# Making the four result fetches of a row wait for each other's landing, in a four-layer kernel's first attention

## The chip, the cores and the metric

The kernel runs on one core of a Trainium2 chip. The metric is the device time of one execution in microseconds (us); the time given for a kernel is the median of its runs.

## The reference, cut to what matters

The input `x` has 16 rows of 256 channels by 512 positions, and `cond` is a 16 x 512 array of zeros and ones. Four layers are added to `x` in turn: an attention with 8 heads (`L0`), a causal convolution along the channel axis with `cond` as its taps, a recurrent layer (a gated cell, 256 steps), and an attention with 16 heads. The first attention is the one of this document:

```python
x = x + _L0_cond_ref(x, cond_2048, L0_cond_Wq, L0_cond_Wo)      # this one
x = x + _L1_cond_ref(x, cond_2048[:, None, :])
x = x + _L2_cond_ref(cond_2048, x, L2_cond_W_ih, L2_cond_W_hh, L2_cond_b_ih, L2_cond_b_hh)
x = x + _L3_cond_ref(x, cond_2048, L3_cond_Wq, L3_cond_Wk, L3_cond_Wv, L3_cond_b)

# inside L0, with cmask/rmask from the mask's columns and rows
logits = (scores * cmask + (1.0 - cmask) * NEG) * rmask
ctx = softmax(logits) @ qh          # keys and values are the queries: one projection
out = ctx @ Wo.T
```

A position whose mask is 0 is never attended to, and as a query it takes the plain mean over all positions. So each row needs its attention only over its positions with mask 1 (under 288 of the 512 here), and one more result, the mean's, for all the others.

## The kernel before

The first attention (`attend0_together`) works on one row (one `b` of 16) after another, packed: it gathers the positions with mask 1 to the front, attends among them, and gives every position its result back. The order of instructions on every engine comes from a planner: each step is added to a plan with an engine, an estimated duration and a place, and the plan puts out a fixed order per engine. Each engine then runs its list in that order, and waits on semaphores where the data asks for it. Rows overlap: while the last steps of row `b` run, the first steps of a later row run between them.

The steps of a row, with their lines:

- `gather`. SyncE loads the row (`xA`, L842). TensorE turns it (L853), ScalarE copies it into `xT` (L857), and POOL sends its positions in four indirect DMAs of 128 positions each to their packed places in a table in HBM (`table<-xT,togo`, L310, function `send`). SyncE fetches the packed table back (`xsA`, L320 and L322). TensorE turns that (L880), projects it (L827, a helper that several products share) and makes values (L914). POOL also makes a mask of places, `uA` (L923).
- `group`, twice, for four heads each. Scores for the row maxima (L938), maxima on VectorE (L945, L950), maxima brought into place by four small DMAs (`whh<-whh`, L957), scores again (L981), exponentials on ScalarE (L990, L993), the weighing (L1011 and L827). The sums of weights go to HBM (L1037).
- `divide`. The sums are loaded (L1041), inverted, stored (L1044), and spread over partitions by eight DMAs (`pbA`, L1051). POOL multiplies the two halves of the context `cxA` by them (L1054).
- `finish`. TensorE multiplies by the output weights (L827 with `woT`), ScalarE copies (L1086), SyncE writes the row's packed results to HBM in two parts (`result<-ocA`, L1091). When both are there, POOL fetches for every position the result that belongs to it, in four indirect DMAs of 128 positions and 128 KB each (`backA<-result,goto`, L1098). VectorE adds all four to `xT` (L1101). Then the first part of the convolution is made from the row's new values: POOL copies them (`early`, L567), VectorE multiplies and sums (L573 to L575).

The plan's order on POOL around the fetches of a row is: four fetches, first scaling of the next row's `cxA`, two sends of a later row, second scaling, third send, `uA`, `early`, fourth send, and then the next row's fetches. From row 10 on there are no sends left. On the SyncE queue, L320 of a later row comes ahead of the two L1091 of the current row.

```python
for f in range(NT):
    outs.append(plan.add("POOL", 1.3, put + (outs[-1:] or [rs_.take(r)]), lambda f=f: nc.gpsimd.indirect_dma_start(
        R4[r.i][:, f], None, results[b], bass.IndirectOffsetOnAxis(goto[:, f, b : b + 1], 0))))
landed = plan.add("LAG", 2.5, outs, lambda: None)
```

In the plan each fetch follows the one before, but only in order: on the chip POOL issues the next as soon as it has issued this one. `R4` (`backA`) has two buffers.

Of the kernel before, what the change touches and what calls it, by code (L numbers as in the profile page):

```python
# [18 lines left out]
B, D, T = 16, 256, 512  # L19
# [245 lines left out]
def tile_kernel(ctx: ExitStack, tc: tile.TileContext, x, cond, Wq0, Wo0, W_ih, W_hh, b_ih, b_hh,  # L265
                Wq3, Wk3, Wv3, b3, consts, out, cols):
    nc = tc.nc
# [296 lines left out]
    def early(b, w, xs, products):  # L564

        if w == 0:
            yield "POOL", 0.7, lambda: nc.gpsimd.tensor_copy(xs[:, :, TAPS - 1 :], xT[:, :, b, 0 : EARLY * PART])  # L567
        a = xs[:, :, w * PART : w * PART + TAPS].unsqueeze(2).broadcast_to([P, NT, PART, TAPS])
        steps = [list(d) for d in a.ap]
        steps[2][0] = 1  # L570
        every = bass.AP(tensor=a.tensor, offset=a.offset, ap=steps)
        y = yw[w // 2][:, :, b, w % 2 * PART : (w % 2 + 1) * PART]
        yield "DVE", 1.3, lambda: nc.vector.tensor_tensor(products, every, condT.unsqueeze(2).broadcast_to([P, NT, PART, TAPS]), ALU.mult)  # L573
        yield "DVE", 1.3, lambda: nc.vector.tensor_reduce(y, products, AX.X, ALU.add)
        yield "DVE", 0.2, lambda: nc.vector.tensor_tensor(y, y, xs[:, :, TAPS - 1 + w * PART : TAPS - 1 + (w + 1) * PART], ALU.add)  # L575
# [155 lines left out]
    def attend0_together():  # L731
# [8 lines left out]
        with ExitStack() as es:  # L740
            work = es.enter_context(tc.tile_pool(name="workA", bufs=1))
            pp = es.enter_context(tc.tile_pool(name="psumA", bufs=1, space=PSUM))
            plan = Plan()
# [28 lines left out]
            def tiles(name, n, shape, space=work):  # L772
                return plan.slots(n), [space.tile(shape, F32, tag=f"{name}{i}", name=f"{name}A{i}") for i in range(n)]
# [20 lines left out]
            rs_, R4 = tiles("back", 2, [P, NT, D])  # L794
            results = [nc.dram_tensor(f"result{b}", (ROOM + 1, D), F32, kind="Internal").ap() for b in range(B)]
            goto = work.tile([P, NT, B], U32, tag="goto", name="goto")
# [26 lines left out]
            def wide(to, left, right, start, stop):  # L823

                n = left.shape[1]
                for r in range(0, n, R):
                    nc.tensor.matmul(to[r : min(n, r + R)], lhsT=left[:, r : min(n, r + R)], rhs=right, start=start, stop=stop, skip_group_check=True)  # L827
# [244 lines left out]
            def finish(b, g0, cx, done):  # L1072

                plan.lay(PLACES["finish"], g0)
                oc, made, put, products = ocs.new(), [], [], []
                for part in range(2):
                    sm = banks.new()

                    def product(part=part, sm=sm):
                        for c in range(2) if part == 0 else [2]:  # L1080
                            r = P if c < 2 else TAILK + 1
                            for g in range(GQ):
                                wide(SM[0:r, sm.i][:, (c % 2) * D : (c % 2 + 1) * D], CX[cx.i][:, g, c * P : c * P + r], woT[:, g, :], g == 0, g == GQ - 1)
                    m = plan.add("PE", 1.71 if part == 0 else 0.86, done + [banks.take(sm)] + ([] if part else [ocs.take(oc)]) + made, product, mode="c32")
                    products.append(m)
                    c = plan.add("ACT", 0.6 if part == 0 else 0.38, [m], lambda part=part, sm=sm: nc.scalar.copy(  # L1086
                        OC[oc.i][:, 0:2].rearrange("p c d -> p (c d)") if part == 0 else OC[oc.i][0 : TAILK + 1, 2],
                        SM[0 : P if part == 0 else TAILK + 1, sm.i][:, 0 : (2 - part) * D]))
                    banks.free(sm, c)
                    made.append(c)  # L1090
                    put.append(plan.add("SP", 3.0, [c], lambda part=part: nc.sync.dma_start(  # L1091
                        out=results[b][0 : 2 * P].rearrange("(c p) d -> p c d", p=P) if part == 0 else results[b][2 * P :],
                        in_=OC[oc.i][:, 0:2] if part == 0 else OC[oc.i][0 : TAILK + 1, 2])))
                cs.free(cx, *products)
                ocs.free(oc, *put)
                r, outs = rs_.new(), []
                for f in range(NT):
                    outs.append(plan.add("POOL", 1.3, put + (outs[-1:] or [rs_.take(r)]), lambda f=f: nc.gpsimd.indirect_dma_start(  # L1098
                        R4[r.i][:, f], None, results[b], bass.IndirectOffsetOnAxis(goto[:, f, b : b + 1], 0))))
                landed = plan.add("LAG", 2.5, outs, lambda: None)  # L1100
                outs = [plan.add("DVE", 1.22, [landed], lambda: nc.vector.tensor_tensor(  # L1101
                    xT[:, :, b], xT[:, :, b], R4[r.i], ALU.add))]
                rs_.free(r, *outs)
                ea, n = ears.new(), None
                for w in range(EARLY if b < B - 1 else 1):
                    for engine, dur, f in early(b, w, *ear):
                        n = plan.add(engine, dur, [n] if n else outs + [ears.take(ea)], f)
                ears.free(ea, n)
                return put
# [9 lines left out]
            for b in range(B):  # L1119
                g0 = GQ * b  # L1120
                v, heads, v_done, turned, u = gather(b, g0)
                cx, done, totals, weighed = cs.new(), [], [], []
                opened = cs.take(cx)
                for g in range(GQ):
                    c, opened, last, tot, summed = group(g, b, g0 + g, heads[g], v, v_done, turned, cx, opened, u)
                    done.append(c)
                    totals.append((tot, summed))
                    weighed.append(last)
                vs.free(v, *weighed)
                us.free(u, *weighed)  # L1130
                put = finish(b, g0, cx, (divide if b < B - 1 else closing)(b, g0, cx, done, totals))
# [643 lines left out]
```

## Time and profile before

| what | value |
|---|---|
| timed runs, us | 2384.07, 2382.76, 2374.28; median 2382.76 |
| the profiled execution's own time | 2376.67 us |
| its span, first to last instruction | 2374.9 us |
| mean granted TensorE clock | 0.971 |
| first attention, fetches of rows 0 to 12 | from 109.34 to 418.40 us |
| fetches of the last three rows | from 440.74 to 467.10 us |
| recurrent layer | until about 1560 us |

How to read it: the profile is one execution. An engine's busy time is the sum of its instructions; semaphores, branches and the issuing of DMAs by SyncE are not in it. For POOL's indirect DMAs the busy time is that of writing the descriptors, about 1 us each, and the data moves after it. The view of waits says for how long an engine stood idle just before an instruction, and which instruction or DMA ended that. The view of the chain goes back from the last instruction, each time to what released it.

### The profile page before, as it was taken

What the parts mean: (1) busy time and instruction counts of PE and PEld (TensorE: products, weight loads), DVE (VectorE), ACT (ScalarE), POOL (GpSimd) and SP (SyncE); (2) the same over time, 40 slices, a digit from 0 to 9 for tenths busy, and PEclk for the clock granted to TensorE, in tenths of its full rate; (3) what the DMA queues carried; (4) which work ended last, traced back from release to release, by engine and by line L of the source; (5) the groups of instructions that cost most, each with busy time, mean ns of one, the idle gap of its engine ahead of it and who ended that gap; (6) DMA issues with size and microseconds to landing.
All of it is one profiled execution on the core that took longest, in us unless ns stands there. A gap on an engine that the chain in (4) does not pass through costs nothing.

```text
span 2374.9 us, 105954 instructions
## 1 busy us (share of the span) xinstructions
PE 2207.9 (93%) x47074; PEld 1460.0 (61%) x47074; DVE 1688.3 (71%) x4639; ACT 995.9 (42%) x2648; POOL 414.0 (17%) x402
## 2 busy tenths in 40 slices
PE   5999999569999999999999999959999999999994
PEld 4555555358989988988898988833333333333331
DVE  2377778768888888888888855666666666666651
ACT  3545544223333333333333333215555555555542
POOL 3244443300000000000000000030332242232113
PEclk8999999789999999999999999989999999999997
DMA  6223322500000000000000000010111111111001
GB/s 202 73 80 89 101 62 63 167 3 4 9 4 5 5 5 5 5 5 4 5 5 5 5 4 4 4 38 15 45 44 32 41 41 40 32 46 36 22 22 40
DMA packets 70166, 83.91 MB, mean 35 GB/s; under 512 B 28808, under 2 KB 48842, under 8 KB 69700
## 3 DMA queue, kind: packets, MB, share of 16 engines
q1 hardware_dynamic: 60484, 60.09, 8.4%
q0 software_dynamic: 9216, 16.96, 2.4%
q8 instruction: 371, 6.08, 1.0%
q14 instruction: 95, 0.78, 0.1%
HBM read 48.58 MB, written 35.98 MB: 36 GB/s over the span
## 4 chain that ended last, share of the span: by engine, by line
PE 88%; DVE 3%; DMA 2%; issue 2%; ACT 2%; POOL 1%; SPq 1%; another core or an unknown queue 0%; POOLq 0%; DVEq 0%; ACTq 0%
PE pr L1211 11%; PE smC L1472 10%; PE pn L1211 9%; PE pz L1211 9%; PE smC L1606 7%; PE smA L827 6%; PE smC L1638 6%; PE smC L1663 5%; PE pt L1202 5%; PE pr L1190 4%; PE pz L1190 4%; PE smA L981 3%; PE smA L1011 3%; PE smA L938 2%; PE smA L853 1%
## 5 line engine op out<-in xcount | busy, mean ns | idle before, releaser
L1613 DVE TENSOR_REDUCE nmC<-smC 128x2 f32<-128x576 f32 x512 | 362.5, 750 | 178.7 <-PE smC L1606 162.2
L310 POOL DMA_INDIRECT table<-xT,togo x128 | 128.1, 1001 | 1239.8 <-DVE whh L1482 1077.3
L1211 PE MATMUL pr<-whh,hist 128*32 128x128 f32 x8192 | 282.8, 275 | 41.7 <-DVE hist L1274 28.9
L1649 ACT ACTIVATE wih<-smC 128x1024 f32<-128x1024 f32 x256 | 251.8, 1023 | 150.4 <-PE smC L1638 149.8
L1211 PEld LDWEIGHTS pr<-whh,hist 128*32 128x32 f32 x8192 | 220.2, 110 | 125.7 <-issue 40.0
L1211 PE MATMUL pz<-whh,hist 128*32 128x128 f32 x8192 | 280.9, 273 | 0.8 <-issue 0.8
L1211 PE MATMUL pn<-whh,hist 128*32 128x128 f32 x8192 | 280.1, 273 | 0.0
L555 DVE SCALAR_TENSOR_TENSOR yw<-xT,condT,yw 128x512 f32<-128x512 f32 x360 | 269.2, 748 | 5.5
L1211 PEld LDWEIGHTS pz<-whh,hist 128*32 128x32 f32 x8192 | 238.6, 110 | 1.6 <-issue 1.2
L1211 PEld LDWEIGHTS pn<-whh,hist 128*32 128x32 f32 x8192 | 238.3, 110 | 0.1
L1190 PE MATMUL pr<-wih,xw 128*32 128x128 f32 x4096 | 225.4, 273 | 3.1 <-issue 3.0
L1190 PE MATMUL pz<-wih,xw 128*32 128x128 f32 x4096 | 226.4, 273 | 1.6 <-issue 1.1
L1245 ACT ACTIVATE nn<-pre 128x64 f32<-128x64 f32 x256 | 65.7, 257 | 385.5 <-DVE pre L1242 385.5
L1606 PE MATMUL smC<-kC,qC 32*128 32x288 f32 x2048 | 200.5, 453 | 7.8 <-ACT wih L1649 2.6
L1606 PEld LDWEIGHTS smC<-kC,qC 32*128 32x128 f32 x2048 | 83.6, 183 | 197.0 <-DVE nmC L1613 82.4
L1236 ACT ACTIVATE r<-pr 128x128 f32<-128x128 f32 x256 | 70.9, 277 | 282.5 <-PE pr L1211 274.7
L1638 PE MATMUL smC<-qC,kC 32*128 32x512 f32 x1024 | 168.2, 638 | 0.2
L1202 PE MATMUL pt<-xw,wih 128*32 128x256 f32 x2048 | 167.7, 379 | 0.1
L1703 POOL TENSOR_TENSOR aC<-aC,pbC 128x512 f32<-128x512 f32 x64 | 81.4, 1279 | 491.3 <-DMA pbC<-sums 420.3
L1190 PEld LDWEIGHTS pz<-wih,xw 128*32 128x32 f32 x4096 | 143.9, 110 | 6.5 <-issue 6.3
L1190 PEld LDWEIGHTS pr<-wih,xw 128*32 128x32 f32 x4096 | 142.9, 110 | 6.2 <-issue 5.6
L1237 DVE STREAM_TRANSPOSE rT<-r 128x128 f32<-128x128 f32 x256 | 78.6, 307 | 76.2 <-ACT r L1236 74.2
(184 smaller groups left out, 3420.8 us busy)
## 6 DMA issues: line engine op xcount, KB each, us to landing
xA<-in_x_dram SPq DMA_DIRECT2D x16, 512.0 KB
pbC<-sums SPq DMA_DIRECT2D x256, 32.0 KB
out_dram<-oC SPq DMA_DIRECT2D x32, 256.0 KB
table<-zeros SPq DMA_DIRECT2D x16, 288.0 KB
pbA<-totals SPq DMA_DIRECT2D x120, 36.0 KB
xsA<-table SPq DMA_DIRECT2D x16, 256.0 KB
result<-ocA SPq DMA_DIRECT2D x16, 256.0 KB
xsC<-table SPq DMA_DIRECT2D x16, 256.0 KB
```

The lines of the kernel that those rows point to most:

```text
L310: one = nc.gpsimd.indirect_dma_start(tables[b], bass.IndirectOffsetOnAxis(togo[:, f, b : b + 1], 0), xT[:, f, b], None, bounds_check=ROOM ...
L555: nc.vector.scalar_tensor_tensor(acc, xT[:, f, :, lo : lo + WIN], condT[:, f, k : k + 1], xT[:, f, :, t0 : t0 + WIN] if k == 0 else acc, A ...
L827: nc.tensor.matmul(to[r : min(n, r + R)], lhsT=left[:, r : min(n, r + R)], rhs=right, start=start, stop=stop, skip_group_check=True)
L1190: nc.tensor.matmul(sets[k % 2][0 if g == GATE_R else 2][32 * j : 32 * j + 32].rearrange("p (f i) -> p f i", i=32), lhsT=x2, rhs=gates(wih, ...
L1202: nc.tensor.matmul(ps[32 * j : 32 * j + 32], lhsT=wih[:, kc, 2 * T + fo * P + 32 * j : 2 * T + fo * P + 32 * j + 32], rhs=parts[p][:, kc]. ...
L1211: nc.tensor.matmul(ps[32 * j : 32 * j + 32].rearrange("p (f i) -> p f i", i=32), lhsT=slot[:, f], rhs=gates(whh, f, j)[:, g], start=False, ...
L1472: nc.tensor.matmul(to[R3 * j : R3 * j + R3], lhsT=left[:, R3 * j : R3 * j + R3], rhs=right, start=start, stop=stop)
L1606: nc.tensor.matmul(SM[:, st[j].i, 0:ROOM], lhsT=Q[qt.i][R * j : R * j + R, qc * P : (qc + 1) * P], rhs=K[kt.i][R * j : R * j + R, 0:ROOM], ...
L1613: nc.vector.tensor_reduce(NM[nm.i][:, qc, lo : lo + len(some)], SM[:, some[0] : some[-1] + 1, 0:ROOM], AX.X, ALU.max, negate=True)
L1638: nc.tensor.matmul(SM[:, st[j].i], lhsT=K[kt.i][r, kc * P : kc * P + P], rhs=Q[qt.i][r, :], start=True, stop=True)
L1649: nc.scalar.activation(E[e.i][:, lo : lo + len(some)], SM[:, some[0] : some[-1] + 1], AF.Exp)
L1663: nc.tensor.matmul(SM[R * j : R * j + R, acc.i], lhsT=V[v.i][:, c, 8 * (g // 2) + 2 * j + q], rhs=E[held[c].i][:, j], start=(c == 0), stop ...
```

## The change

The four fetches of a row get a wait. Each but the first is made to depend on the landing of the one asked for before it, in rows 0 to 12; in rows 13, 14 and 15 nothing changes. The plan's steps, durations and places are the same, and so is the order of all instructions on every engine; what differs in the built program are the semaphores that these POOL instructions wait for.

```diff
                 r, outs = rs_.new(), []
+                fetched = []
+
+                def bring(f):
+                    one = nc.gpsimd.indirect_dma_start(R4[r.i][:, f], None, results[b], bass.IndirectOffsetOnAxis(goto[:, f, b : b + 1], 0))
+                    if fetched and b < B - 3:
+                        tc.add_manual_dep(one.ins, fetched[-1].ins.name, mybir.DependencyInfo(mybir.DependencyClass.Sync, mybir.DependencyReason.DATA),
+                                          reason="one part of a row's results is fetched when the part that was asked for last is there")
+                    fetched.append(one)
                 for f in range(NT):
-                    outs.append(plan.add("POOL", 1.3, put + (outs[-1:] or [rs_.take(r)]), lambda f=f: nc.gpsimd.indirect_dma_start(
-                        R4[r.i][:, f], None, results[b], bass.IndirectOffsetOnAxis(goto[:, f, b : b + 1], 0))))
+                    outs.append(plan.add("POOL", 1.3, put + (outs[-1:] or [rs_.take(r)]), lambda f=f: bring(f)))
                 landed = plan.add("LAG", 2.5, outs, lambda: None)
```

## The prediction

> **What bounds the kernel now.** I read the page first, then the first attention alone (about 45 to 440 us of the span), because nothing after it is edited. The page has TensorE on top:
>
> ```profile
> PE 2207.9 (93%) x47074; PEld 1460.0 (61%) x47074; DVE 1688.3 (71%) x4639; ACT 995.9 (42%) x2648; POOL 414.0 (17%) x402
> ```
>
> In the ten rows whose fetches begin between 109.34 and 339.00 us (0 to 9, to the next row's at 366.56) TensorE is busy 93% too, and POOL 45%. A share is no limit, so the next view is POOL's timeline over one row (columns: start, duration, engine, line, tiles, and in brackets the idle time before it and what ended it):
>
> ```profile
> 213.26 1.98 POOL L1098 DMA_INDIRECT backA<-result,goto  x1 [7.84 <-DMA result<-ocA]
> 215.55 0.97 POOL L1098 DMA_INDIRECT backA<-result,goto  x1 [0.30 <-issue]
> 216.82 0.95 POOL L1098 DMA_INDIRECT backA<-result,goto  x1 [0.30 <-issue]
> 218.08 0.95 POOL L1098 DMA_INDIRECT backA<-result,goto  x1 [0.30 <-issue]
> 219.64 0.79 POOL L1054 TENSOR_TENSOR cxA<-cxA,pbA 128x288 f32<-128x288 f32 x1 [0.60 <-issue]
> 223.07 1.03 POOL L310 DMA_INDIRECT table<-xT,togo  x1 [2.64 <-ACT xT L857]
> ...
> 229.50 1.06 POOL L310 DMA_INDIRECT table<-xT,togo  x1 [0.17 <-issue]
> 238.53 1.20 POOL L1098 DMA_INDIRECT backA<-result,goto  x1 [7.96 <-DMA result<-ocA]
> ```
>
> Four fetches 0.30 us apart; the first scaling of `cxA`; 2.64 us of waiting for ScalarE; the four sends with the second scaling, `uA` and `early` among them; then 8 us until the next row's results are in HBM. That last wait looks like room, but the SyncE queue says otherwise. Its timeline behind the last send:
>
> ```profile
> 232.07 0.71 SPq L320 DMA_DIRECT2D xsA<-table  x1
> 232.88 1.16 SPq L957 DMA_DIRECT2D whh<-whh  x2
> 234.14 0.39 SPq L1091 DMA_DIRECT2D result<-ocA  x1
> 234.58 1.14 SPq L957 DMA_DIRECT2D whh<-whh  x2
> 235.77 0.43 SPq L322 DMA_DIRECT2D xsA<-table  x1
> 236.31 0.31 SPq L1091 DMA_DIRECT2D result<-ocA  x1
> ```
>
> The last send ends at 230.56 and its packets land at 231.58. L320 needs it, so it goes at 232.07; both L1091, which write the results, stand behind L320 in the same queue without a break; the second lands and the next fetch starts at 238.53. So there is a ring: fetches, scaling, sends, L320, L1091, next row's fetches. A row can be no shorter than one turn. The waits from 100 to 360 us tell how much of a turn is slack (columns: waiter, releaser, us in total, times, longest):
>
> ```profile
> POOL table L310 <- ACT xT L857: 35.3, 10, 6.7
> POOL uA L923 <- PE smA L827: 6.9, 10, 1.4
> ...
> SPq L320 <- DMA table<-xT,togo: 18.0, 10, 2.9
> ```
>
> In all ten rows SyncE stands at L320 until the sends are there, so every row goes through the ring. The first two lines are POOL waiting for other engines inside it: that time can be used up before a row grows.
>
> **The turn of the ring before.** Row 0's first fetch starts at 109.34 and row 10's at 366.56: 257.2 us, 25.7 a row. Slack: 35.3 less ten times the 0.17 us that an unwaited instruction shows, 33.6; for `uA` 6.9 - 1.7 = 5.2; the 0.60 ahead of a scaling: together 39.4. From the last send's end to the next first fetch it takes 7.71 to 9.23 us, 8.3 on average; I count 0.3 a row of that as slack too. In all 42 us, 4.2 a row.
>
> **What the change adds.** No instruction is added, taken away or moved on any engine; the second, third and fourth fetch of rows 0 to 12 each gain a wait for the landing of the one before, 39 waits. They stand on POOL, and behind a waiting fetch are queued both scalings (TensorE's output products at L827 wait for them), the sends (L320), `uA` and `early`.
>
> Price of one wait. The trace has no fetch that waits for a fetch. It has sends of the same kind that wait for a send, in the last attention:
>
> ```profile
> POOL table L310 <- DMA table<-xT,togo: 76.2, 42, 3.2
> ```
>
> There the packets land 0.97 us after the instruction's end (median) and POOL starts again 0.6 us later, 1.56 of idle instead of 0.30. A fetch lands later than a send: by the DMA packets of the thirteen rows the first one's last packet comes 2.45 us after its instruction's end, the second's 2.20, the third's 2.01, the fourth's 1.76 (medians; the fourth has least beside it). Lower bound: every wait costs the send's 1.56, so three add 3 x 1.26 = 3.8 us a row. Upper bound: every one costs 2.45 + 0.6 = 3.05, 3 x 2.75 = 8.25 us. I take the fetches' own rows, with the hop of 0.6: 3.0 for the first, which still meets the load of `x` and the spreads of `pbA` issued around it; 2.3 each for the second and third, which would be alone as the fourth now nearly is. That is 7.6 - 0.9 = 6.7 us a row.
>
> Sum: ten rows of 6.7 are 67, less 42 of slack: **25 us** late. Bounds: 38 - 42, so nothing; 82.5 - 39.4 = 43. Rows 10 to 12 have no sends behind them: only the scalings are late, the two of row 10 ending at 374.23 where TensorE takes them at 380.00, row 11's at 395.65 for 403.18, row 12's at 420.28 for 427.2. 5.8 to 7.5 us of cover against 6.7: up to 1 us, in row 10. The last three rows keep their fetches as they are, and everything from there on is shifted whole.
>
> What else stands behind the waits and hides: VectorE's L1101 (adding the results) waits for the fourth landing, which comes at about 2.3 us after that fetch; the second scaling comes 4.2 us after it, so TensorE is held by the scaling first. `early` goes out later and VectorE's products (L573) with it; VectorE is busy 74% here and has the next row's 4 us before its row maxima are needed; I count zero. If that cover fails, it falls inside the same turn, since L320 is later still.
>
> The profiled execution took 2376.67 us (span 2374.9 and 1.8 around it), 6 below the median of the three timed ones, 2382.76. All four average 2379.4; with 25 that is **2404 us**.
>
> **Rivals.** *Faster: spaced fetches stop slowing TensorE.* The chain from 205 to 245 us has the scores of a row's first group beside its second group's (start, us, what):
>
> ```profile
> 205.98 2.19 PE smA L981 x32
> ...
> 216.93 3.08 PE smA L981 x32
> 220.01 0.02 issue
> 220.03 0.66 ACT wih L993
> ```
>
> The same 32 records take 2.19 us without fetches and 3.08 with them, and the weighing that follows starts at 220.73 for L993; measured from a row's first L880, that weighing comes at 3.39 us in the row begun at 64.9, which has no fetch, and at 4.2 to 7.7 in the eleven rows from 109.8 on, 25 us in all. Half-clock stretches of 3.4 us follow some of those stalls. If the burst is the cause and spacing cures it, TensorE's row falls from 25.7 to about 23.4, for thirteen rows 30 us: 2350. Against it: the ring must turn faster too, and even with the lower bound it turns in 21.5 + 3.8 = 25.3. It decides only if a wait costs under about 1.2 us, less than any wait of this kind in the trace, or if the ring is not closed as I read it. 10%.
>
> The Trainium skill, in "SBUF — State Buffer", section "Who interferes with whom", says that DMA never contends with a compute engine. By that rule this rival is worth 0, by the row above up to 30; the forecast needs neither.
>
> *No change: the slack swallows it.* A wait near the send's price, or a return path with more slack than 0.3 a row; 2372 to 2391. For it: POOL idles over half of the row. Against it: fetches land later than sends in every row. 18%.
>
> *Slower by more: TensorE, now waiting for scalings, loses its clock.* Some of its stops of 2 us and more are followed by 3.4 us at half clock, 1.7 us each; over ten rows 17 on top, or landings at the upper bound: 2422. Part of the 72% for slower. That the waits do nothing can be set aside: the built program shows a landing's semaphore on each of the 39.
>
> **How the numbers follow.** Slower 72%, no change 18%, faster 10%, with 0.5% (12 us), about what a measurement can tell, as the line. The forecast's own range is 2393 to 2422. To leave out no more than 2 in 10 the range goes down through the unchanged cases to 2377, and up to the upper bound, 2422.
>
> **What would show it.** Right: second to fourth fetches with idle of 2.2 to 3 us released by a DMA of `backA`; the waits of L310 for ScalarE and of `uA` for TensorE near nothing; first fetches about 28 us apart in rows 1 to 8; TensorE at L827 waiting for POOL's `cxA`; time after 440 us unchanged but shifted by some 25. Wrong: first fetches under 25.5 us apart; waits of under 1.5 us; L981 in the fetch rows back at 2.2 us with the rows shorter.

## The result: slower by 51 us, twice the forecast

| | before | after |
|---|---|---|
| median of the timed runs, us | 2378.52 (2372.55 to 2384.07, 4 runs) | 2429.72 (2422.94 to 2435.64, 4 runs) |
| ratio, 95% interval | | 1.0226, 1.0205 to 1.0246 |
| profiled execution's span, us | 2374.9 | 2428.4 |
| first fetch of row 0, row 10, row 13, us | 109.34, 366.56, 440.74 | 108.30, 408.80, 487.87 |

The direction was right and the size was not: 2404 was forecast, and the time lies above the range. When row 13 begins the kernel after is 47 us late, and all of that comes from rows 0 to 12, since row 0 had begun 1 us earlier than before. In the kernel after, the lines behind the changed place have moved: L1098 is L1100, L1101 is L1108. TensorE's busy time rose by 13 us (its line on the page; 2207.9 before), though it does the same work; its granted clock in the first attention is lower too, as a later section shows.

```profile
PE 2220.8 (91%) x47074; PEld 1459.6 (60%) x47074; DVE 1684.1 (69%) x4639; ACT 996.3 (41%) x2648; POOL 424.0 (17%) x402
```

POOL's timeline over one row, to set beside the one of before (start, duration, engine, line, tiles; in brackets the idle time before it and what ended it):

```profile
228.77 1.21 POOL L1100 DMA_INDIRECT backA<-result,goto  x1 [7.87 <-issue]
233.81 1.34 POOL L1100 DMA_INDIRECT backA<-result,goto  x1 [3.83 <-DMA backA<-result,goto]
237.44 0.95 POOL L1100 DMA_INDIRECT backA<-result,goto  x1 [2.30 <-DMA backA<-result,goto]
241.05 0.95 POOL L1100 DMA_INDIRECT backA<-result,goto  x1 [2.65 <-DMA backA<-result,goto]
242.03 0.80 POOL L1054 TENSOR_TENSOR cxA<-cxA,pbA 128x288 f32<-128x288 f32 x1
243.00 1.04 POOL L310 DMA_INDIRECT table<-xT,togo  x1 [0.17 <-issue]
244.34 1.87 POOL L310 DMA_INDIRECT table<-xT,togo  x1 [0.30 <-issue]
...
249.56 2.02 POOL L310 DMA_INDIRECT table<-xT,togo  x1 [0.17 <-issue]
260.13 1.00 POOL L1100 DMA_INDIRECT backA<-result,goto  x1 [8.55 <-DMA result<-ocA]
```

Three waits of 3.83, 2.30 and 2.65 us where there were 0.30; the 2.64 us of waiting for ScalarE ahead of the first send are gone; and, which nobody had asked for, two of the four sends take 1.87 and 2.02 us instead of 1.00 and 1.06. Behind the last send the SyncE queue has the same closed order as before:

```profile
254.01 0.38 SPq L320 DMA_DIRECT2D xsA<-table  x1
254.50 1.16 SPq L957 DMA_DIRECT2D whh<-whh  x2
255.76 0.39 SPq L1091 DMA_DIRECT2D result<-ocA  x1
256.20 1.14 SPq L957 DMA_DIRECT2D whh<-whh  x2
257.39 0.43 SPq L322 DMA_DIRECT2D xsA<-table  x1
257.93 0.31 SPq L1091 DMA_DIRECT2D result<-ocA  x1
```

The waits from 100 to 390 us say who stands now (waiter, releaser, us in total, times, longest):

```profile
POOL backA L1100 <- DMA backA<-result,goto: 84.2, 29, 5.4
...
PE smA L827 <- POOL cxA L1054: 47.4, 18, 3.7
```

TensorE, which had no wait for `cxA` here, stops for both scalings of nearly every row. L310's wait for ScalarE and `uA`'s for TensorE are no longer among the waits. The queue's own waits over the same stretch show SyncE standing longer for the sends, 89.3 us where the prediction read 18.0 (from 100 to 360 us):

```profile
SPq L320 <- DMA table<-xT,togo: 89.3, 18, 8.3
```

So the ring of the prediction is what turns; where its turn is longer than the sum, the next table says.

**The ten turns, term by term.** Sums over rows 0 to 9, read from POOL's timeline:

| term, us over ten rows | before | after | difference | forecast |
|---|---|---|---|---|
| idle ahead of the second fetch | 3.06 | 36.97 | +33.9 | +27 |
| ahead of the third | 3.05 | 24.90 | +21.9 | +20 |
| ahead of the fourth | 3.06 | 24.64 | +21.6 | +20 |
| second send, second scaling, fourth send: their own duration | 29.02 | 45.62 | +16.6 | 0 |
| idle ahead of first scaling, first send and `uA` | 42.97 | 2.38 | -40.6 | -39.4 |
| last send's end to the next first fetch | 83.14 | 77.22 | -5.9 | -3 |
| all the rest | 92.92 | 88.77 | -4.2 | 0 |
| row 0's first fetch to row 10's | 257.22 | 300.50 | +43.3 | +25 |

From row 10's first fetch to row 13's it is 74.18 us before and 79.07 after: 4.9 more, where at most 1 was forecast.

### The profile page after: what moved, and what is told of

Its sections match the earlier page's. It is cut to its first block, busy times and chain, and to the rows that moved or that the text cites. A ratio compares the mean times of both kernels' runs of the same rounds, so it can differ in the third digit from the quotient of the medians.

```text
span 2428.4 us, 105971 instructions
## 1 busy us (share of the span) xinstructions
PE 2220.8 (91%) x47074; PEld 1459.6 (60%) x47074; DVE 1684.1 (69%) x4639; ACT 996.3 (41%) x2648; POOL 424.0 (17%) x402
## 4 chain that ended last, share of the span: by engine, by line
PE 80%; issue 6%; DMA 5%; DVE 3%; POOL 3%; ACT 2%; SPq 1%; POOLq 0%; another core or an unknown queue 0%; DVEq 0%; ACTq 0%
PE smC L1479 11%; PE pr L1218 10%; PE pn L1218 9%; PE pz L1218 9%; PE smC L1613 7%; PE smC L1645 6%; PE smC L1670 5%; PE pt L1209 5%; PE pr L1197 4%; PE pz L1197 4%; PE smA L827 4%; DMA backA<-result,goto 2%; PE smA L981 2%; DMA result<-ocA 1%; POOL backA L1100 1%
## 5 line engine op out<-in xcount | busy, mean ns | idle before, releaser
L310 POOL DMA_INDIRECT table<-xT,togo x128 | 142.6, 1114 | 1212.5 <-DVE whh L1489 1086.3
```

Of the source, the lines that this page charges most:

```text
L310: one = nc.gpsimd.indirect_dma_start(tables[b], bass.IndirectOffsetOnAxis(togo[:, f, b : b + 1], 0), xT[:, f, b], None, bounds_check=ROOM ...
```

## The experiments

They came in four sets, each on one chip together with the kernel before; the second and the fourth set were on the same chip. That kernel took 2340.34, 2340.66, 2374.27 and 2341.60 us in them; the pair above, at 2378.52, is like the third. Gains and losses are therefore always taken against the kernel before of the same set. "Quiet" below means the chips with 2340 us.

### First set: parts of the change (kernel before 2340.34 us, 13 runs)

**One wait a row.**

```diff
-                    if fetched and b < B - 3:
+                    if f == 2 and b < B - 3:
```

> Only the third fetch of a row waits (for the landing of the second), in rows 0 to 12; the four go in two pairs. Theory A (POOL's turn decides, with about 4.2 to 4.8 us of slack a row): one wait of 2.9 us instead of 0.3 stays inside the slack, rows keep 25.7 us or less, time about 2378, and less if a pair disturbs TensorE less than a burst of four. Rival B (each wait costs its share of the 51 us, through TensorE and VectorE standing behind it): a third of it, about 2396. In both the wait itself is 2.3 to 3.0 us.

Measured: 2357.78, ratio 1.0075 (1.0058 to 1.0092), 17 us slower: to the microsecond what rival B said. Neither theory had expected that the kernel before would be 38 us faster here. The trace shows where the 17 us are: the ten turns take 244.27 us, 24.4 a row, with 3.2 us of idle ahead of the third fetch, against 229.11 us in the trace of the kernel before that the second set gives. That fits the sum once the slack is small, but this run alone does not exclude rival B; the kernels of the second and third set do.

**The sends' duration.** `dust` is a new tile of four columns.

```diff
+        def multiply():
+            if w == 0 and b < B - 1:
+                nc.vector.tensor_reduce(dust, xs[:, :, TAPS - 1 : TAPS - 1 + EARLY * PART], AX.X, ALU.add)
+            nc.vector.tensor_tensor(products, every, condT.unsqueeze(2).broadcast_to([P, NT, PART, TAPS]), ALU.mult)
-        yield "DVE", 1.3, lambda: nc.vector.tensor_tensor(products, every, ...)
+        yield "DVE", 1.3, multiply
```

> All 39 waits stay. VectorE gets one small reduction of early (about 0.3 us) ahead of its first multiplication (L573 of the kernel after), so that this starts after POOL has begun the fourth send of a row, not 0.14 us before it. Theory A (a send of 1.0 us takes 2.0 when VectorE's two-input multiplication has begun just before it): the fourth sends go back to 1.0 to 1.1 us, the ten turns from 300.5 to about 291, time about 2420. Rival B (a send takes 2.0 because its own transfers or its descriptors meet other traffic): sends stay at 2.0, time 2430 or a little more.

Measured: 2411.57, ratio 1.0305 (1.0287 to 1.0322); ten turns in 288.07 us, 12.4 less than in the kernel after, where 9.5 were expected. The ten fourth sends take 1.06 us each, 10.62 in sum instead of 20.23. The second send, which VectorE's L1108 meets, was left alone and still takes 2 us in some rows (four sends of 1.98 to 2.05). First the kernel after, fourth send and VectorE beside it:

```profile
249.42 1.22 DVE L573 TENSOR_TENSOR products<-early,condT 128x1024 f32<-128x1024 f32 x1 [2.46 <-POOL early L567]
```

against the send at 249.56 shown above: VectorE is 0.14 us ahead, and the send takes 2.02. With the reduction between (L578 is that kernel's L573):

```profile
246.51 1.06 POOL L310 DMA_INDIRECT table<-xT,togo  x1 [0.17 <-issue]
```
```profile
246.37 0.42 DVE L577 TENSOR_REDUCE dust<-early 128x4 f32<-128x256 f32 x1 [2.46 <-POOL early L569]
246.71 1.22 DVE L578 TENSOR_TENSOR products<-early,condT 128x1024 f32<-128x1024 f32 x1
```

The send is 0.20 us ahead of the multiplication, and takes 1.06. The reduction, which has one input, stands 0.14 us ahead of it and does not lengthen it. In the kernel before the send of the row shown in the prediction stood at 229.50 and VectorE followed at 229.88. So the order in which the send and the multiplication start decides, by a tenth of a microsecond. In the kernel after 15 of the 40 sends take 1.87 to 2.04 us, all of them with such a VectorE instruction over them, and no send without one takes more than 1.04.

**The last three rows alone.**

```diff
-                    if fetched and b < B - 3:
+                    if fetched and 10 <= b < B - 3:
```

> The waits only in rows 10, 11 and 12, which have no sends behind them. Theory A (the loss is made in POOL's turn of rows 0 to 9; in the last rows only VectorE's addition and the scalings come later): 0 to 5 us, time 2378 to 2384. Rival B (each row with waits costs the same, 51 / 13 = 3.9 us): 12 us, time 2390.

Measured: 2352.59, ratio 1.0056 (1.0037 to 1.0075), 12 us: again rival B's number. The trace, beside that of the kernel before in the second set, puts it into single rows: from one first fetch to the next, row 10 takes 23.54 us instead of 18.08, row 11 22.58 instead of 21.86, row 12 32.74 instead of 25.19. Row 12 of this kernel on POOL:

```profile
378.12 1.04 POOL L1100 DMA_INDIRECT backA<-result,goto  x1 [7.17 <-DMA result<-ocA]
384.39 1.59 POOL L1100 DMA_INDIRECT backA<-result,goto  x1 [5.23 <-issue]
388.26 0.95 POOL L1100 DMA_INDIRECT backA<-result,goto  x1 [2.28 <-DMA backA<-result,goto]
392.86 0.96 POOL L1100 DMA_INDIRECT backA<-result,goto  x1 [3.65 <-DMA totals<-totA]
393.84 1.54 POOL L1054 TENSOR_TENSOR cxA<-cxA,pbA 128x288 f32<-128x288 f32 x2
```

Waits of 5.23 and 3.65 us: loads of weights are issued beside the first and the third fetch, at 377.27 and 388.13. But the load is not all of the 5.23: the first fetch's last packet lands 2.81 us after the fetch's end, and POOL starts only 2.4 us behind it, where 0.6 to 0.8 is usual. At this same fetch the kernel before stands 1.99 us instead of 0.30 with no landing to wait for, in the first pair as in the second set; what stops POOL there stays open. TensorE takes the scaled `cxA` at 394.69; in the second set's kernel before it takes it at 387.51, 3.3 us after the scalings' end at 384.20 (2.5 us in row 10, 6.2 in row 11). VectorE also stands, 7.5 us at L1108, but the chain that ends row 12 goes through the scaling. So the theory was right that there is no turn here, and wrong on the cover: it was 2.5, 6.2 and 3.3 us, not 5.8, 7.5 and 6.9. The time of 12 us is outside its 0 to 5. Of the 13.7 us that the rows show, 9.9 are left when row 13 begins, because the earlier rows were a little shorter (2344.09 and 2344.17 us are the whole times of these two executions: what lies behind row 13 scatters by about as much).

**One fetch instead of four.** The second to fourth fetch of rows 0 to 12 are left out, and `backA` is cleared once. What VectorE then adds is not the whole result, so this kernel serves for its times alone.

```diff
                 def bring(f):
+                    if f and b < B - 3:
+                        return
...
+                nc.vector.memset(R4[i], 0.0)
```

> The kernel before with the second to fourth fetch of rows 0 to 12 left out (backA is cleared once instead, and VectorE adds what lies there). Theory A (the burst of four fetches is what delays the exponentials and the weighing behind it): the first exponential of the second group comes 2.5 us after a row's first L880 in every row, as in the rows without fetches, against 3.4 to 5.7 before; a row takes about 23.4 us, time about 2350. Rival B (the delay comes from the loads, the spreads or the sends around it, or from TensorE itself): it comes as late as before, and the time falls only by what POOL's three issues of 1.25 us free in its turn, which has slack already: about 2378.

Measured: 2337.92, ratio 0.9993 (0.9980 to 1.0006): no difference. The first exponential came at 2.53 us in every row but the first, whose start takes longer in all kernels, and so it did in the kernel with one wait and in rows 0 to 9 of the one above, which have the full burst. On this chip there was nothing to cure.

### Second set: both kernels once more (kernel before 2340.66 us, 7 runs)

> The kernel before, unchanged, for its trace beside the next ones. Theory A (the burst of four fetches held TensorE back in the first pair of runs, and did not in the experiments so far, where rows 0 to 9 with the burst took 22.7 us each): either rows of 22.7 us, the first exponential at 2.53 us after the row's first L880, and about 2340 us; or, where the disturbance is there, rows of 25.7, 3.4 to 5.7 us, and about 2378. Rival B (the disturbance was an accident of one execution): rows of 22.7 whatever the total.

> The kernel after, unchanged. Theory A (POOL's turn with three waits takes 30.0 us whatever TensorE does): first fetches 30.0 us apart here too, so a loss of 10 x (30.0 - 22.7) + 5 = 78 us where the kernel before has rows of 22.7, and of 51 where it has rows of 25.7. Rival B (the waits cost what they cost, a fixed 51 us): 51 us in both.

The kernel before took 2344.17 (one run), with the first exponential at 2.52 or 2.53 us there too; so the chip is a quiet one, and this trace cannot tell whether the disturbance of the first pair was an accident of one execution. The seven runs of the third set, all from 2367 to 2381 us, show that it was not. The kernel after took 2427.29, ratio 1.0362 (1.0339 to 1.0386), 87 us slower. So the kernel after costs the same as in the first pair, 2429.72, and its ten turns are the same, 300.39 us against 300.50; what differs between chips is the kernel before. TensorE's share says it best (from:to, length, then busy time of PE; the clock is the third number from the end). The kernel before in the first pair:

```profile
109.00:366.00 257.00, 239.07 (x3136) 134.72 (x3136) 190.64 (x333) 131.92 (x299) 115.52 (x120) 0.97 0.30 85
```

the same kernel here:

```profile
109.00:366.00 257.00, 257.00 (x3586) 142.68 (x3588) 222.69 (x383) 148.09 (x335) 140.39 (x133) 1.00 0.34 92
```

and the kernel after, first pair:

```profile
109.00:366.00 257.00, 212.93 (x2676) 112.87 (x2676) 160.41 (x281) 113.21 (x255) 107.34 (x102) 0.89 0.26 74
```

Here the kernel before keeps TensorE busy without a gap, and a row takes 22.69 us from one first L880 to the next (22.9 on average between first fetches). POOL has next to no slack in that: its waits ahead of the first scaling, the first send and `uA` are 6.0 us over ten rows instead of 43.0. The three waits add 78 us (9.2 to 87.4), as they add 77 in the first pair, and here the ten turns grow by 71.3; 14.0 more come in rows 10 to 12. Rival B, a fixed 51 us, is out.

The one-wait kernel with the late multiplication (the two edits above together):

> Only the third fetch waits, and VectorE's first multiplication starts a little later, so that it does not stretch the fourth send. Theory A: the turn of 24.4 us that one wait alone gave falls by the 1.0 us that each fourth send was stretched, to 23.4 to 23.7; against rows of 22.7 that is a loss of 8 to 10 us, against rows of 25.7 a gain of about 20. Rival B (the 17 us that one wait cost come from the wait and VectorE behind it, not from the turn): a loss of 17 us or more.

Measured: 2354.63, ratio 1.0057 (1.0035 to 1.0078), 14 us; ten turns in 238.89 us. The interval, 8 to 18 us, holds both expectations, so only the trace tells: 9.8 us are in the ten turns, as theory A has it, and 5.3 in rows 10 to 12, which it had left out. The fourth sends are back at 10.6 us in sum, and the row fell from 24.4 to 23.9, half of what each send gave back. The rows still lie above the 22.69 of TensorE.

> The kernel before with the second to fourth fetch of rows 0 to 12 left out, beside a trace of the kernel before on the same chip. Theory A: rows of 22.7 us with the first exponential at 2.53; so no gain where the kernel before has such rows itself, and a gain of about 30 us where its rows take 25.7. Rival B (the burst has no part in it): the same rows as the kernel before, whichever they are.

Measured: 2336.86 (one run), 4 us below, rows of 22.69: as expected where nothing disturbs TensorE.

### Third set: a chip like that of the first pair (kernel before 2374.27 us, 7 runs)

**The same time on POOL, without a wait.**

```diff
                     fetched.append(one)
+                    if f == NT - 1 and b < B - 3:
+                        for _ in range(10):
+                            nc.gpsimd.memset(idle, 0.0)
```

(`idle` is a tile of 800 columns, and no fetch waits.)

> The kernel before (four fetches in a burst, no waits), with ten clearings of a scratch tile on POOL behind the fourth fetch of rows 0 to 12, about 0.76 us each, 7.6 us in all: as much time as the three waits put into POOL's turn (78 us over ten rows), but every fetch is issued and landed as early as before. Theory A (the time on POOL ahead of the scalings and sends is the loss): rows 29.5 to 30 us, loss 75 to 85 us against rows of 22.7. Rival B (the loss comes from VectorE and TensorE standing behind a late fourth landing): rows of 22.7 to 24, loss under 15 us. Should the kernel before show rows of 25.7 on this chip, it also tells whether a burst holds TensorE back (first exponential later than 2.53 us) where TensorE has time to spare.

Measured: 2430.86, ratio 1.0239 (1.0209 to 1.0270), 57 us slower, ten turns in 303.35 us. The kernel after, on a chip like this, is 51 us slower with 300.50. A row on POOL:

```profile
202.18 0.99 POOL L1101 DMA_INDIRECT backA<-result,goto  x1 [7.62 <-DMA result<-ocA]
203.48 0.96 POOL L1101 DMA_INDIRECT backA<-result,goto  x1 [0.31 <-issue]
...
206.00 1.81 POOL L1101 DMA_INDIRECT backA<-result,goto  x1 [0.30 <-issue]
207.82 8.19 POOL L1108 MEMSET idleA<- 128x800 f32 x10
215.98 0.79 POOL L1055 TENSOR_TENSOR cxA<-cxA,pbA 128x288 f32<-128x288 f32 x1
```

Nothing waits for a landing, the results land early, and the loss is there: 8.2 us of POOL's time ahead of the scaling and the sends. Rival B, with under 15 us, is out. The second thing in this kernel: it has the burst, and TensorE, which has time to spare, is delayed all the same. Its ScalarE, in the row whose first L881 (before: L880) starts at 203.31:

```profile
208.38 2.28 ACT L994 ACTIVATE wih<-smA 128x576 f32<-128x576 f32 x4 [1.26 <-PE smA L982]
```

The exponential comes 5.07 us after the row's start; in the twelve rows of TensorE that begin beside a burst it comes at 2.56 to 5.41.

**Two waits.**

```diff
-                    if fetched and b < B - 3:
+                    if f > 1 and b < B - 3:
```

> The third and the fourth fetch wait, the second does not. Theory A (the turn is a sum): the 30.0 us of three waits less the 3.4 us of the first landing, 26.6 us a row, and a tail of 5 us instead of 10: a loss of 10 x (26.6 - 22.7) + 5 = 44 us. Rival B (each wait costs the same third of the 87 us): 58 us.

Measured: 2396.54, ratio 1.0095 (1.0063 to 1.0126), 22 us. Both expectations were reckoned for rows of 22.7; against rows of 25.7 the sum would have said 10 x (26.6 - 25.7) + 5 = 14, a third of 51 for each wait 34. The kernel before has no trace in this set; 25.7 us and the 257.22 us of its ten turns are those of the first pair. The ten turns took 274.08, 27.4 a row: 0.8 above the sum, because the second fetch, now issued in a pair with the first, landed later and the third waited 3.25 us for it instead of 2.49. With 27.4 the sum is 10 x 1.7 + 5 = 22, but that it meets the measured 22 is partly luck: the 5 us for rows 10 to 12 are not in the trace (72.71 us there, against 74.18 in the first pair's kernel before). The 17 of the ten turns can be read from the traces; what lies behind row 13 scatters by about as much as the rest.

> Second to fourth fetch of rows 0 to 12 left out once more, for a chip on which the kernel before has rows of 25.7 us. Theory A (the burst of fetches holds TensorE back there): rows of 22.7 and some 30 us less than the kernel before; on a chip where the kernel before has rows of 22.7, no difference. Rival B (something else there does): the rows stay as long as the kernel before has them.

Measured: 2342.58 (one run), 32 us below the kernel before. The row that begins at 203.94:

```profile
206.46 2.28 ACT L994 ACTIVATE wih<-smA 128x576 f32<-128x576 f32 x4 [0.59 <-PE smA L982]
```

2.52 us after its first L881, and 2.52 or 2.53 in every row of this kernel. This kernel also has fewer fetches; but the one with two waits, on the same chip and with all four, has its first exponential at 2.52 to 2.95 us, and the kernel after of the first pair at 2.53. So on this kind of chip it is the burst, and not the number of fetches, that holds TensorE back. Without it the kernel takes some 32 us less (one run, against seven from 2367 to 2381).

### Fourth set (kernel before 2341.60 us, 7 runs)

> One wait a row (the third fetch) with VectorE's first multiplication a little later, for a chip on which the burst holds TensorE back. Theory A: POOL's turn stays at 23.9 us as measured before, and two pairs leave the first exponential at 2.5 to 3.0 us; so where the kernel before takes about 2375, rows of 25.7, this is 10 x (25.7 - 23.9) = 18 us faster less 3 for the tail, about 2360; where the kernel before takes about 2340, 14 us slower as before. Rival B (a wait costs time on any chip): 14 us slower in both.

Measured: 2354.25, ratio 1.0063 (1.0046 to 1.0080), 13 us; ten turns in 236.93 us. The chip was a quiet one, so this repeats the 14 us of the second set. Whether this kernel gains the 15 us that the sum gives it on a chip where the burst disturbs TensorE was not seen. No kernel here beat the kernel before of its set, but for those that leave fetches out.

## Why the prediction was wrong

**Right: the ring.** Rows 0 to 9 are one turn of POOL and the SyncE queue, the waits stand inside it, and TensorE's, VectorE's and the later rows' work follows. The kernel that only keeps POOL busy shows that this time is the loss. The slack was used up as forecast: idle time that was 42.97 us fell to 2.38.

**Wrong, the largest term: "no instruction is added" was read as "no instruction gets longer".** The sends and the second scaling grew by 16.6 us over ten rows, 9.6 of them in the fourth sends. In the first pair the waits brought POOL's instructions and VectorE's L573 and L1108 to the same moments. The row shown in the prediction had the send 0.38 us ahead of L573, a closeness that was there to be seen. The upper bound of 43 us left this term out, and with it the range.

**Wrong: the price of a wait.** 6.7 us a row was put in, 7.73 came: 3.70, 2.49 and 2.46 us of idle instead of 3.0, 2.3 and 2.3. The first landing was mis-sized most: in rows 0 to 7, where the load of `x` is issued 0.8 to 1.3 us ahead of that fetch, the wait is 3.06 to 5.38 us, 4.0 on average; in rows 8 and 9, which have no such load, 2.48 and 2.49. The second set's trace of this kernel shows the same (3.9 us on average in rows 0 to 7; 2.71 and 3.06). No run took the load away alone, so that it is the cause is argued from this. I had allowed for that load with 3.0. Together this is 10 us of the 18 that the ten turns missed.

**Wrong: the cover of rows 10 to 12.** Forecast up to 1 us, 4.9 came in the first pair and 14.0 on a quiet chip. The waits there were taken at the usual price, but in row 12 two of the three are longer (4.24 and 3.94 us in the kernel after, 5.23 and 3.65 in the kernel with waits in rows 10 to 12 alone), beside loads of weights and a stop of POOL that the kernel before has too. And the 5.8 to 7.5 us of cover were read from a chip whose TensorE was late; on a quiet chip the cover is 2.5, 6.2 and 3.3.

**Wrong the other way:** the return path gave 5.9 us of slack, not 3, and the fetches' own durations and the rest fell by 4.2. Added up: 10.3 + 16.6 - 1.2 - 2.9 - 4.2 = 18.6 us, and with the forecast's 67 - 42.4 = 24.6 the 43.3 of the table but for rounding.

**Not the change:** the profiled pair differs by 53.5 us, and 47 are there at row 13. The recurrent layer accounts for 9.1 (1055.8 and 1064.9 us from its first to its last step), the last attention for -2.7. In the traces of the experiments that layer takes 1057 to 1064 us, 1063.9 in the kernel before and 1063.6 in the kernel after of the second set. It is scatter of one execution, and the timed medians differ by 51.2.

**The slack itself belonged to the chip.** The 42 us that I took off are the time for which a TensorE disturbed by the burst let POOL wait. On a quiet chip the same change costs 87 us, since a row there is 22.7 us and POOL's turn already about as long. The stretched sends belonged to the chip as well: in the second set's kernel before, without any wait, VectorE's L573 starts 0.12 to 0.14 us ahead of the fourth send in nine of the ten rows, and these sends already take 2.02 us (19.25 in sum, 20.23 in the kernel after). Second send, second scaling and fourth send together grow by only 2.9 us over ten rows there, instead of 16.6.

**The rivals.** *Faster* had the mechanism right and the outcome wrong: spacing does cure the delay (2.53 us in all rows of the kernel after), worth some 32 us where there is one, by the kernel with one fetch. But the ring with three waits turns in 30 us, and the gain goes to a TensorE that now waits 47 us for `cxA`. *Slower by more, by the clock:* the clock did fall, from 0.97 to 0.89 in the stretch shown above, with 64.9 us at half clock between 109 and 440 us instead of 20.5. It is not in the turn: the stretch from the last send to the next fetch, in which TensorE's products lie, became shorter. *No change* needed as much slack as the waits cost, 77 us; 46.5 was there (40.6 and 5.9).

The rule of the Trainium skill in "SBUF — State Buffer", section "Who interferes with whom", that DMA never contends with a compute engine, was set against the row of 3.08 us. The quiet chips side with the rule (-2.4 us without three of four fetches), the third set with the row (-31.7 us), though what TensorE waits for there stays open.

## What to carry to other kernels

A wait in a closed ring costs its whole time as soon as the slack is gone, so first ask whose delay made the slack; if it is a disturbance that the change removes, it is no slack. A wait also moves instructions against those of other engines, and durations change with that: look for pairs that start within half a microsecond of each other, and price both orders. And a proportional rival can hit the numbers twice, as it did in the first set; only the trace and a case far from the others (the quiet chip, the busy POOL) told it apart.

## What the runs showed of the hardware

**A two-input VectorE instruction that starts first holds back POOL's indirect DMA.** 128 x 1024 in f32, 1.22 us; begun 0.14 us ahead it makes a send of 1.0 us take 2.02, begun 0.2 us behind it the send takes 1.06. The Trainium skill, in "SBUF — State Buffer", section "Who interferes with whom", says that issue order decides who blocks, and there the runs agree. It also infers that `tensor_tensor` does not stall the making of descriptors; there the measurement differs, at least for these indirect DMAs. A send also takes its places from a tile, `togo`; which of its steps waits, the runs do not show.

**A burst of four indirect fetches delays TensorE's scores and the exponentials behind them in some sets of runs and not in others.** The same program takes 2340 and 2375 us; with one fetch of four it takes 2338 and 2343. The fetches land no later where TensorE is delayed (medians of the first to fourth, from the fetch's end to its last packet, 2.45, 2.20, 2.01, 1.76 us in the kernel before of the first pair, 2.65, 2.27, 1.96, 2.00 in the quiet one of the second set), so it is not slower fetches. What the delayed engines wait for stays open, and so does what sets the sets apart: the four ran on three chips, and the one that was used twice was quiet both times, but nothing else was varied.
